# Decoder layer with routed experts: routing's normalisation written two half batches later, full-array matmuls written ahead of the values, zero rows written one transfer at a time

## The chip, the core and the metric

The kernel runs on one core of a Trainium2 chip. The metric is the device time of one execution in microseconds; the time before is the median of three runs.

## The reference

One pre-norm decoder layer on 64 sequences of 128 tokens of width 128, in float32. Two attention blocks with 16 heads of width 8 (self attention, and cross attention over a context of 77 tokens) are followed by a mixture of 8 experts, of which each token uses the best two:

```python
x = x + attn(layernorm(x))                     # 16 heads of 8
x = x + xattn(layernorm(x), ctx, mask)         # 77 keys, mask of ones
x = x + ffn(layernorm(x))

def ffn(x):                                    # E = 8, F = 512, top 2
    proj = x @ Wp.T
    gate = l2norm(proj) @ l2norm(sim).T / temperature
    top_v, top_i = top_k(gate, 2)
    comb = sum(one_hot(top_i) * softmax(top_v)[..., None], axis=-2)
    h = gelu(einsum('bsd,edf->ebsf', x, W1) + b1)
    eo = einsum('ebsf,efd->ebsd', h, W2) + b2
    return einsum('ebsd,bse->bsd', eo, comb)
```

## The kernel before

**Stages.** The 64 sequences form 16 groups of four (a sequence is called a batch in the code). First comes attention: 16 jobs of self attention and then 16 of cross attention, one job a group, 128 batches in all, in one software pipeline. Then `experts` computes the expert products for the rows of groups 0 to 10 (part 0, 51 tiles of 256 rows), and once more for groups 11 to 15 (part 1, 27 tiles). Results are gathered back and added (`gather`); the gathers of part 0 run beside the products of part 1.

**The pipeline of attention.** Step s has two halves, called half batches here. In each half `score_tiles` (S) computes two of the four head groups of batch s as scores with queries on the partitions (`ps`), and two head groups of batch s - 4 as scores with keys on the partitions (`pt`), with matmuls of 32 rows that alternate. DVE takes the row maxima `m` from `ps` (L648); they are transposed (`pm`, L659) and brought by DMA into a spare row of the queries (`qh<-md`), so that `pt` comes out shifted, and ACT takes its exponential `e` (L675). `values` (V, L690) multiplies `e` of batch s - 5 with the values, and in the other half with ones to get the sums; in every second step DVE takes the reciprocal of the sums and the product (L698, L699). `ps` and `pt` have two PSUM banks each: the next S starts when the maxima and exponentials of the last are done.

Besides S and V, each half holds some full-array matmuls, called F here: one item of the queue `todo` (taken by `next_`) and at most one of the queue `late`. `todo` holds the prologue of a job that is one to two groups ahead (normalise, transpose, query, key, value), the transposing of maxima (`turn`) and the output projection of two batches (`project`, `py`, L707). The prologue's normalise has no matmul: POOL subtracts and scales (`xn`, L170), and in self attention also takes the inverse root of the variance behind DVE's statistics (L148, L149). A group's `project` comes twice (p = 0 and 1); after p = 1 of either attention come the residual sum `xs` (L711), the statistics (L148, L149) and POOL's inverse root `rstd` (`root`, L154 to L158).

**Routing.** After p = 1 of a cross group, `route(g)` gives a function `norm` and four steps. `norm` is four DVE instructions (L170, tile `x`, buffers `x3`), called at once. The steps are queued in `late` with due times of 3, 4, 6 and 8 half batches: `trans` (transposes, an ACT copy), `project` (`pp`, squares on ACT, inverse root on POOL), `choose` (`pg`, a run of small DVE instructions for the best two), `place` (`pr`, the rows' slots). `place` fills `sending` with eight scatters, of which each half takes one: an indirect DMA of POOL that writes 128 rows into the expert rows `xr` in DRAM, written to follow the newest exponential.

When the last group of a part is placed, `table` computes from the counts which expert each tile of 256 rows belongs to and where each expert's rows end (`tail`), and then writes 256 zero rows behind the end of each of the 8 experts: a register load on SP and a DMA from `zero_s`, eight times. For part 0 this is in attention; for part 1 it is in the first expert stage, where the remaining steps of the last group are run by the function `more`, one item every second tile.

**Order.** TensorE's (PE's) instructions run in the order in which the code writes them (`manual_schedule`). The order of the others is drawn up when the program is compiled, from dependences and estimated times; the written order decides between those that are ready. In `experts` each tile's row fetch on SP is placed behind the last SP transfer of the same chain (`behind("SP")`), as are the zero writes:

```python
with behind("SP"):
    row = nc.sync.value_load(part.row[0:1, t : t + 1], ...)
i = nc.sync.dma_start(v["x"], part.x[bass.ds(row, TILE), :]...)
after(i.ins, part.scatters)
last["SP"] = i.ins
```

Rows are fetched three tiles ahead of their product.

Of the kernel before, what the change touches and what calls it, by code (L numbers as in the profile page):

```python
# [8 lines left out]
F32 = mybir.dt.float32  # L9
# [13 lines left out]
NEG = -(2.0 ** 100)  # L23
LAG = 4
TILE = 256
LATER = (3, 4, 6, 8)
SPLIT = 11


# [1 line left out]
def decoder_layer(  # L31
# [217 lines left out]
    def route(g):  # L249
# [121 lines left out]
            after(i.ins, behind)  # L371
            part.scatters.append(i.ins)

        def table():

            pn = ps_m.tile([P, E], F32, tag="mm", name="pn")
            nc.tensor.matmul(pn, ones_f, part.seen, start=True, stop=True)
            M = part.rows // TILE
            N = part.tiles
            over = hp.tile([P, E, M], F32, tag="over", name="over", bufs=1)  # L380
            need = hp.tile([P, M], F32, tag="need", name="need", bufs=1)
            nc.vector.tensor_scalar(need, tid[:, :M], float(TILE), None, ALU.mult)
            count = hp.tile([P, E], F32, tag="count", name="count", bufs=1)
            nc.vector.tensor_copy(count, pn)
            nc.vector.tensor_tensor(
                over, count.unsqueeze(2).to_broadcast([P, E, M]),
                need.unsqueeze(1).to_broadcast([P, E, M]), ALU.is_gt,
            )
            nt = hp.tile([P, E], F32, tag="nt", name="nt", bufs=1)
            nc.vector.tensor_reduce(nt, over, AX.X, ALU.add)  # L390
            acc = hp.tile([P, E, E], F32, tag="acc", name="acc", bufs=1)
            nc.vector.tensor_tensor(
                acc, low, nt.unsqueeze(1).to_broadcast([P, E, E]), ALU.mult
            )
            end = hp.tile([P, E], F32, tag="end", name="end", bufs=1)
            nc.vector.tensor_reduce(end, acc, AX.X, ALU.add)
            past = hp.tile([1, N, E], F32, tag="past", name="past", bufs=1)
            nc.vector.tensor_tensor(
                past, tid[:1, :N].unsqueeze(2).to_broadcast([1, N, E]),
                end[:1].unsqueeze(1).to_broadcast([1, N, E]), ALU.is_ge,  # L400
            )
            ex = hp.tile([1, N], F32, tag="ex", name="ex", bufs=1)
            nc.vector.tensor_reduce(ex, past, AX.X, ALU.add)
            nc.vector.tensor_tensor(
                past, past, nt[:1].unsqueeze(1).to_broadcast([1, N, E]), ALU.mult
            )
            be = hp.tile([1, N], F32, tag="be", name="be", bufs=1)
            nc.vector.tensor_reduce(be, past, AX.X, ALU.add)
            nc.vector.tensor_tensor(be, tid[:1, :N], be, ALU.subtract)
            nc.vector.tensor_scalar(be, be, float(TILE), None, ALU.mult)  # L410
            rw = hp.tile([1, N], F32, tag="rw", name="rw", bufs=1)
            nc.vector.tensor_scalar(rw, ex, float(part.step), None, ALU.mult)
            nc.vector.tensor_tensor(rw, rw, be, ALU.add)
            part.row = hp.tile([1, N], I32, tag=f"prow{part.n}", name="prow", bufs=1)
            nc.vector.tensor_copy(part.row, rw)
            nc.vector.tensor_scalar(ex, ex, float(E - 1), float(WE), ALU.min, ALU.mult)
            part.wat = hp.tile([1, N], I32, tag=f"pwat{part.n}", name="pwat", bufs=1)
            nc.vector.tensor_copy(part.wat, ex)

            nc.vector.tensor_tensor(count, count, part.base, ALU.add)  # L420
            tail = hp.tile([1, E], I32, tag=f"tail{part.n}", name="tail", bufs=1)
            nc.vector.tensor_copy(tail, count[:1])
            for e in range(E):
                with behind("SP"):
                    r = nc.sync.value_load(
                        tail[0:1, e : e + 1], min_val=e * part.step,
                        max_val=e * part.step + part.rows,
                    )
                i = nc.sync.dma_start(
                    part.x[bass.ds(r, TILE), :].rearrange("(h p) d -> p h d", p=P), zero_s  # L430
                )
                last["SP"] = i.ins
                apart(i.ins, f"x{part.n}")
                part.scatters.append(i.ins)

            K = part.last - part.first
            every = slice(part.first * GB, part.last * GB)
            less = hp.tile([P, E], F32, tag="less", name="less", bufs=1)  # L440
            nc.vector.tensor_scalar(
                less, nt, -float(TILE), float(part.step), ALU.mult, ALU.add
            )
            sf = slot_f[:, every, :].rearrange("p b k -> p (b k)")
            off = hp.tile([P, 2 * GB * SPLIT], F32, tag="off", name="off")[:, : 2 * GB * K]
            one = hp.tile([P, 2 * GB * SPLIT], F32, tag="one", name="one")[:, : 2 * GB * K]
            nc.vector.tensor_copy(off, sf)
            for e in range(1, E):
                nc.vector.tensor_scalar(
                    one, sf, float(e * part.step), less[:, e - 1 : e], ALU.is_ge, ALU.mult  # L450
                )
                nc.vector.tensor_tensor(off, off, one, ALU.subtract)
            nc.vector.tensor_copy(back[:, every, :].rearrange("p b k -> p (b k)"), off)

        return norm, [trans, project, choose, place], table if g == part.last - 1 else None

    last, newest, sending = {}, [None], []

    def behind(engine):
        return tc.issue_after(last[engine]) if engine in last else nullcontext()  # L460
# [14 lines left out]
    def attention():  # L475
        jobs = [(cross, g) for cross in (False, True) for g in range(NGRP)]
        NB = len(jobs) * GB
        with (
# [222 lines left out]
            def project(n, p):  # L701
                cross, g = jobs[n]
                v = G[n]
                wo_ = co_s if cross else wff_s
                py = ps_m.tile([P, 2, D], F32, tag="mm", name="py")
                for k in range(2):
                    nc.tensor.matmul(  # L707
                        py[:, k, :], v["aT", p][:, k, :], wo_, start=True, stop=True
                    )
                at = slice(2 * p, 2 * p + 2)  # L710
                nc.vector.tensor_tensor(xs[g][:, at, :], py, xs[g][:, at, :], ALU.add)  # L711
                if p == 1:
                    stats(g)
                    root(g)
                    v.clear()
                    if cross:
                        norm, steps, table = route(g)
                        norm()
                        late.extend((now[0] + w, f) for w, f in zip(LATER, steps))
                        if table:  # L720
                            late.append((0, table))

            loads(0)
            for f in prologue(0):
# [8 lines left out]
            for s in range(NB + LAG + 3):  # L733
                a, t, z = s, s - LAG, s - LAG - 1
                if s % GB == 2 and s // GB + 2 < len(jobs):
                    todo += prologue(s // GB + 2)
                if s == GB:
                    load_experts()
                do_a, do_t = a < NB, t in range(NB)
                for half in range(2):  # L740
                    far = (0, 1) if half == 0 else (2, 3)
                    near = (2, 3) if half == 0 else (0, 1)
                    score_tiles(a if do_a else None, far, t if do_t else None, near)
                    for x, y in zip(far, near):
                        if do_a:
                            maxima(a, x)
                        if do_t:
                            exps(t, y)
                    if z in range(NB):
                        values(z, half == 1)  # L750
                    next_()

                    now[0] += 1
                    if late and late[0][0] <= now[0]:
                        late.pop(0)[1]()
                    if sending:
                        sending.pop(0)([newest[0]])
                if len(todo) > 4:
                    next_()
                if a < NB and a % 2:  # L760
                    todo.insert(0, lambda n=a // GB, p=a % GB // 2: turn(n, p))
                if z in range(NB) and z % 2:
                    todo.insert(1, lambda n=z // GB, p=z % GB // 2: project(n, p))
# [113 lines left out]
    with tc.manual_schedule(engines={mybir.EngineType.PE}):  # L877
# [3 lines left out]
        with (  # L881
# [4 lines left out]
            def more(t):  # L886
                if rest and t % 2 == 1:
                    rest.pop(0)()
                if sending:
                    sending.pop(0)([newest[0]])  # L890

            experts(parts[0], ff, ps_h, ps_y, more)
            assert not rest and not sending
            done = [(g, b) for g in range(SPLIT) for b in range(GB)]

            def some(t):
# [68 lines left out]
```

## Time and profile before

| | |
|---|---|
| Median of 3 runs | 1540.02 us (1536.16 to 1541.31) |
| Profiled execution | 1553.91 us, of which the span is 1552.2 |
| Mean granted TensorE clock | 0.887 |
| PE busy in the span | 1301.2 us (84%) |
| DVE, ACT, POOL busy | 757.7, 530.0, 578.5 us |

By stage, from windows of the profile:

| Stage | us | PE busy | DVE busy | POOL busy | granted clock |
|---|---|---|---|---|---|
| self attention, 99 to 491 | 392 | 379.05 | 272.36 | 132.21 | 1.00 |
| cross attention, 491 to 1106 | 615 | 543.99 | 294.55 | 266.10 | 0.87 |
| experts of part 0, 1106 to 1310 | 204 | 195.72 | 81.25 | 15.71 | 0.97 |
| experts of part 1 and gathers, 1310 to 1552 | 242 | 126.72 | 77.89 | 124.62 | 0.74 |

Rows of a timeline or of the waits give the start and length in us, the engine, the line of the kernel, the operation, output and input tiles, the shapes and the number of merged instructions; in brackets stands how long the engine was idle just before and who released it. Ends of matmuls are modelled. A row of windows gives the stretch, its length, then for PE, its weight loads, DVE, ACT and POOL the busy time with the number of instructions, and at the end the granted clock, the DMA engines' busy share and GB/s.

### The profile page before, as it was taken

The page shows a single profiled execution, that of the slowest core. Times are in us where ns is not written, and L with a number is a line of the kernel's source. Part 1 is how long each engine was busy: PE and PEld are TensorE (multiplying, and loading weights), DVE is VectorE, ACT ScalarE, POOL GpSimd, SP SyncE. Part 2 cuts the span into 40 slices and gives each one's busy share as a digit, 9 for nine tenths or more (in the row PEclk, how much of TensorE's full clock was granted, in tenths as well). Part 3 has the DMA queues.
Part 4 walks back from the last instruction along what each step waited for, and adds up shares of the span by engine and source line. Part 5 has one row for each costly group of instructions (what it writes and reads, how often), then busy time and mean ns, then how long its engine had stood idle before and what let it go on. Part 6 is the DMA issues. An engine that isn't in the chain of part 4 may idle for free.

```text
span 1552.2 us, 47623 instructions
## 1 busy us (share of the span) xinstructions
PE 1301.2 (84%) x20147; PEld 1032.1 (66%) x20147; DVE 757.7 (49%) x2094; ACT 530.0 (34%) x1167; POOL 578.5 (37%) x928
## 2 busy tenths in 40 slices
PE   1889999999999999999999998988679999555940
PEld 1667777777777666666666666666579999444840
DVE  2347767767765454444444445444343333333422
ACT  1134444444444333333333333323334444111410
POOL 5404243342523244444444443334410001666136
PEclk9589999999999899898989898878789999687975
DMA  7542212122221111111111112101132222333212
GB/s 196 132 91 52 53 40 60 40 53 50 43 53 40 34 45 47 48 47 46 47 44 49 42 47 69 39 16 36 41 94 75 69 75 73 89 90 93 83 51 71
DMA packets 120213, 95.58 MB, mean 62 GB/s; under 512 B 22584, under 2 KB 102592, under 8 KB 120000
## 3 DMA queue, kind: packets, MB, share of 16 engines
q1 hardware_dynamic: 97328, 58.73, 15.5%
q0 software_dynamic: 8192, 16.79, 3.8%
q10 hardware_dynamic: 14480, 17.02, 3.6%
q8 instruction: 158, 2.59, 0.7%
q14 instruction: 55, 0.45, 0.1%
HBM read 49.60 MB, written 42.89 MB: 60 GB/s over the span
## 4 chain that ended last, share of the span: by engine, by line
PE 68%; POOL 11%; issue 7%; DVE 6%; DMA 4%; another core or an unknown queue 2%; SPq 1%; POOLq 0%; ACT 0%; DVEq 0%
PE po L690 14%; PE ps L629 13%; PE py L824 7%; PE ph L806 7%; PE pt L629 4%; PE pt L638 4%; PE py L707 3%; PE ps L638 3%; POOL rstd L154 3%; POOL xn L170 3%; POOL r L858 2%; PE pq L567 2%; PE pv L593 2%; PE pk L579 2%
## 5 line engine op out<-in xcount | busy, mean ns | idle before, releaser
L675 ACT ACTIVATE e<-pt 128x512 f32<-128x512 f32 (+1 forms) x512 | 279.2, 592 | 382.1 <-PE pt L638 236.3
L629 PE MATMUL ps<-kh,qh 31*128 31x128 f32 (+1 forms) x4096 | 346.1, 299 | 64.2 <-DVE m L648 51.3
L648 DVE TENSOR_REDUCE m<-ps 128x4 f32<-128x512 f32 (+1 forms) x512 | 275.8, 578 | 252.8 <-PE ps L638 125.6
L629 PEld LDWEIGHTS ps<-kh,qh 31*128 31x128 f32 x4096 | 294.2, 202 | 136.1 <-DVE m L648 82.2
L629 PE MATMUL pt<-qh,kh 32*128 32x128 f32 (+1 forms) x4096 | 334.5, 293 | 7.0 <-DMA qh<-md 5.2
L629 PEld LDWEIGHTS pt<-qh,kh 32*128 32x128 f32 (+1 forms) x4096 | 268.5, 173 | 11.3 <-issue 10.1
L858 POOL DMA_INDIRECT r<-yr,back x128 | 124.6, 974 | 257.0 <-DMA xr<-xr 150.7
L365 POOL DMA_INDIRECT xr<-x,slot x128 | 129.0, 1008 | 236.0 <-ACT e L675 148.9
L813 ACT ACTIVATE hT<-ph,wr 128x256 f32<-128x256 f32 x312 | 128.9, 471 | 248.0 <-issue 227.2
L806 PE MATMUL ph<-xT,wr 128*128 128x256 f32 x624 | 162.2, 407 | 27.8 <-DVE xT L798 11.6
L824 PE MATMUL py<-wr,hT 128*128 128x128 f32 x1248 | 164.2, 283 | 24.7 <-issue 24.4
L824 PEld LDWEIGHTS py<-wr,hT 128*128 128x128 f32 x1248 | 160.7, 200 | 33.7 <-issue 29.0
L690 PE MATMUL po<-e,ones_w 128*32 128x128 f32 (+1 forms) x4096 | 155.5, 292 | 2.6 <-issue 1.8
L806 PEld LDWEIGHTS ph<-xT,wr 128*128 128x128 f32 x624 | 121.1, 204 | 46.7 <-DVE xT L798 12.8
L690 PE MATMUL po<-e,vm 128*32 128x128 f32 (+1 forms) x4096 | 141.9, 278 | 1.3 <-issue 1.1
L690 PEld LDWEIGHTS po<-e,ones_w 128*32 128x32 f32 (+1 forms) x4096 | 113.9, 116 | 39.9 <-issue 31.3
L698 DVE RECIPROCAL aT<-po 128x256 f32<-128x256 f32 x64 | 112.5, 1757 | 41.1 <-PE po L690 40.2
L690 PEld LDWEIGHTS po<-e,vm 128*32 128x32 f32 (+1 forms) x4096 | 105.4, 110 | 31.2 <-issue 24.0
L170 POOL TENSOR_SCALAR xn<-xs,stat,rstd 128x128 f32<-128x128 f32 x128 | 103.6, 818 | 56.3 <-PE tp L184 54.4
L830 DVE TENSOR_TENSOR yr<-py,wr 128x256 f32<-128x256 f32 x78 | 33.0, 424 | 179.4 <-PE py L824 140.0
L163 POOL TENSOR_SCALAR var<-stat 128x4 f32<-128x4 f32 x48 | 11.3, 235 | 259.2 <-DVE stat L149 257.3
L638 PE MATMUL pt<-ident_b,bias 128*77 128x512 bf16 x256 | 100.3, 408 | 0.0
(163 smaller groups left out, 1383.5 us busy)
## 6 DMA issues: line engine op xcount, KB each, us to landing
xr<-xr SPq DMA_DIRECT2D x78, 128.0 KB
yr<-yr SPq DMA_DIRECT2D x78, 128.0 KB
d<-qT ACTq DMA_DIRECT2D x32, 256.0 KB
qh<-d SPq DMA_DIRECT2D x128, 64.0 KB
xs<-in_x_dram SPq DMA_DIRECT2D x16, 256.0 KB
d<-kT ACTq DMA_DIRECT2D x16, 256.0 KB
kh<-d SPq DMA_DIRECT2D x64, 64.0 KB
we_s<-in_w_dram SPq DMA_DIRECT2D x16, 256.0 KB
```

The costliest lines, as they stand in the source:

```text
L170: (engine or nc.gpsimd).tensor_scalar(xn[:, b, :], xs[g][:, b, :], stat[:, i, 0:1], rstd[:, i : i + 1], ALU.subtract, ALU.mult,)
L365: i = nc.gpsimd.indirect_dma_start(out=part.x, out_offset=bass.IndirectOffsetOnAxis(ap=slot[:, g * GB + b, k : k + 1], axis=0), in_=v["xn" ...
L629: nc.tensor.matmul(pt[:, r, :], v[still][rows, r, b, :], v[moving][rows, r, b, :], start="bias" not in v or r == 0, stop="bias" not in v,)
L638: nc.tensor.matmul(pt, left, right.unsqueeze(1).to_broadcast([P, HG, K]), start=False, stop=True,)
L648: nc.vector.tensor_reduce(v["m", b // 2][:, c, :, b % 2], v.pop(("ps", b, c)), AX.X, ALU.max, negate=True,)
L675: i = nc.scalar.activation(e[:K], pt[:K], AF.Exp)
L690: nc.tensor.matmul(po[32 * c : 32 * c + 32, :], w[:, 32 * j : 32 * j + 32], v["e", b, c][:K, j, :], start=(j == 0), stop=(j == HG - 1),)
L698: nc.vector.reciprocal(r, v["o"][:, 1])
L806: nc.tensor.matmul(ph[:, c % 2, :], v["w"][:, c * P : (c + 1) * P], v["xT"], start=True, stop=True,)
L813: i = nc.scalar.activation(v["h"][:, n, :], ph[:, n % 2, :], AF.Gelu, bias=v["w"][:, WF + n : WF + n + 1],)
L824: nc.tensor.matmul(py[:, h, :], v["h"][:, c, h * P : (h + 1) * P], v["w"][:, F + c * D : F + (c + 1) * D], start=(c == 0), stop=(c == NFC ...
L858: inst = nc.gpsimd.indirect_dma_start(out=r, out_offset=None, in_=part.y, in_offset=bass.IndirectOffsetOnAxis(ap=back[:, i, k : k + 1], ax ...
```

## The change

Three edits. First, `norm` is no longer called at once after `project`, but becomes the first of five entries in `late`, with a due time of 2 half batches; since the queue is looked at right after the count goes up, it is written one half after the projection, behind that half's scores and `next_`. Second, in each half `values` moves behind `next_` and the item of `late`: S V F becomes S F V. Third, `table` becomes a function of its own outside `route`, and its eight zero writes go into a new queue `clearing`, of which each half (and in `more` each tile) takes one. The computations of `table` are the same; its text is only moved.

```diff
-LATER = (3, 4, 6, 8)
+LATER = (2, 3, 4, 6, 8)
...
+        return [norm, trans, project, choose, place]
+
+    def table(part):
...
-            for e in range(E):
-                with behind("SP"):
-                    r = nc.sync.value_load(
-                        tail[0:1, e : e + 1], min_val=e * part.step,
-                        max_val=e * part.step + part.rows,
-                    )
-                i = nc.sync.dma_start(
-                    part.x[bass.ds(r, TILE), :].rearrange("(h p) d -> p h d", p=P), zero_s
-                )
-                last["SP"] = i.ins
-                apart(i.ins, f"x{part.n}")
-                part.scatters.append(i.ins)
+        def tail_zeros(e):
+            with behind("SP"):
+                r = nc.sync.value_load(
+                    tail[0:1, e : e + 1], min_val=e * part.step,
+                    max_val=e * part.step + part.rows,
+                )
+            i = nc.sync.dma_start(
+                part.x[bass.ds(r, TILE), :].rearrange("(h p) d -> p h d", p=P), zero_s
+            )
+            last["SP"] = i.ins
+            apart(i.ins, f"x{part.n}")
+            part.scatters.append(i.ins)
+
+        clearing.extend(lambda e=e: tail_zeros(e) for e in range(E))
...
-        return norm, [trans, project, choose, place], table if g == part.last - 1 else None
-
-    last, newest, sending = {}, [None], []
+    last, newest, sending, clearing = {}, [None], [], []
...
                     if cross:
-                        norm, steps, table = route(g)
-                        norm()
-                        late.extend((now[0] + w, f) for w, f in zip(LATER, steps))
-                        if table:
-                            late.append((0, table))
+                        late.extend((now[0] + w, f) for w, f in zip(LATER, route(g)))
+                        if g == parts[g >= SPLIT].last - 1:
+                            late.append((0, lambda: table(parts[g >= SPLIT])))
...
-                    if z in range(NB):
-                        values(z, half == 1)
                     next_()
 
                     now[0] += 1
                     if late and late[0][0] <= now[0]:
                         late.pop(0)[1]()
+                    if z in range(NB):
+                        values(z, half == 1)
                     if sending:
                         sending.pop(0)([newest[0]])
+                    if clearing:
+                        clearing.pop(0)()
...
                 if sending:
                     sending.pop(0)([newest[0]])
+                if clearing:
+                    clearing.pop(0)()
```

## The prediction

> **What bounds it now.** I read the waits first, then the timelines of DVE and PE around one of them, then windows of the granted clock, then SP. The waits of the whole span name one chain:
>
> ```profile
> DVE x L170 <- POOL rstd L158: 48.2, 16, 8.7
> PE ps L629 <- DVE m L648: 51.3, 30, 6.1
> ```
>
> Routing's normalisation x waits 16 times, once a cross group, for POOL's inverse root; PE's scores wait for the maxima m. DVE, then PE, in group 5 show that it is one chain:
>
> ```profile
> 707.43 0.42 DVE L711 TENSOR_TENSOR xs<-py,xs 128x256 f32<-128x256 f32 x1 [2.45 <-PE py L707]
> ...
> 711.21 1.12 DVE L170 TENSOR_SCALAR x<-xs,stat,rstd 128x128 f32<-128x128 f32 x4 [2.61 <-POOL rstd L158]
> 712.24 0.86 DVE L648 TENSOR_REDUCE m<-ps 128x4 f32<-128x308 f32 x2
> ```
> ```profile
> 709.75 0.28 PE L659 MATMUL pm<-ident,m 128*32 128x128 f32 x1
> 712.77 0.34 PE L629 MATMUL ps<-kh,qh 31*128 31x77 f32 x1 [2.74 <-DVE m L648]
> ```
>
> DVE is in order: m stands behind x, and PE idles 2.74 us. The windows (PE busy second, granted clock third from the end) show the larger price:
>
> ```profile
> 712.00:713.00 1.00, 0.23 (x4) 0.23 (x4) 1.00 (x4) 0.00 (x0) 0.80 (x1) 0.98 0.00 0
> 713.00:714.00 1.00, 1.00 (x20) 0.96 (x21) 0.10 (x1) 0.00 (x0) 0.00 (x0) 0.50 0.26 82
> ...
> 723.00:724.00 1.00, 1.00 (x12) 0.41 (x11) 0.51 (x2) 0.29 (x1) 0.00 (x0) 0.90 0.00 0
> ```
>
> From 712.98 to 723.2 PE runs at half clock. Every cross group repeats this: groups 1 to 10 have periods of 38.0 to 40.2 us (mean 39.2), a gap of 2.74 (group 1: 3.03), then 6.8 or 10.2 us at half clock. The longer phase makes the period 1.75 us longer for 3.4 us more of half clock, so the loss is 0.51 of it: 4.3 us on average. The clock changes only on a grid of 3.41 us. Which idle time trips it:
>
> ```profile
> 552.50:555.90 3.40, 2.08 (x38) 1.24 (x37) 0.87 (x5) 1.34 (x3) 1.99 (x6) 1.00 0.26 63
> 555.90:559.30 3.40, 1.68 (x34) 1.49 (x35) 1.93 (x6) 0.00 (x0) 1.20 (x2) 1.00 0.10 29
> 559.40:562.80 3.40, 3.40 (x38) 2.24 (x37) 1.15 (x3) 1.19 (x2) 0.96 (x1) 0.50 0.02 6
> ```
>
> 1.32 us idle in one grid window kept the clock, 1.72 in the next lost it; a gap of 1.69 at 1403.4, all in one window, kept it. So some 1.7 us, half a window, decides.
>
> The Trainium skill (TensorE: Matmul & The Clock Gate, Part 1) has the free-running window of about 3.4 us, but asks for a whole idle window or a gap over some 3 us. By that 2.74 us would cost no clock and the cross part below would be 13 x 1.5 = 20 us instead of 73; the trace, with a drop after every 2.74, decides against it.
>
> The second wait lies in the first expert stage:
>
> ```profile
> 1133.25 8.83 SPq L429 DMA_DIRECT2D xr<-zero  x8
> 1142.91 0.40 SPq L780 DMA_DIRECT2D xr<-xr  x1
> ```
> ```profile
> 1145.24 0.66 PE L796 MATMUL tp<-ident,xr 128*128 128x128 f32 x2 [7.95 <-DMA xr<-xr]
> ```
>
> Eight zero writes go ahead of a row fetch on SP, and PE waits 7.95 us.
>
> **Does x move?** PE follows the written order; the other engines' order is drawn up at compile time by readiness. The self stage proves it:
>
> ```profile
> 266.52 0.27 DVE L148 BATCH_NORM_STATS2 st<-xs 128x6 f32<-128x128 f32 x1
> 266.70 0.30 DVE L149 BATCH_NORM_AGGREGATE stat<-st 128x2 f32<-128x6 f32 x2
> 266.92 1.25 DVE L648 TENSOR_REDUCE m<-ps 128x4 f32<-128x512 f32 x2
> ```
>
> Of the eight statistics of a period, four belong to a prologue written after these maxima and the next ones, and still run ahead of both. x needs only xs, its statistics and rstd, nothing from the halves that it is moved past. So I expect x to stay ahead of m: the new due time does nothing by itself. No instruction is added or removed anywhere.
>
> **Part 1: full-array work F ahead of the values V.** Cross halves go from S V F to S F V. Between py (the p = 1 projection) and the second score block after it stands one V more (1.01 us), so POOL gets that lead. Counted from the end of py's own score block (704.57): now py at 1.0, xs at 2.86, x at 6.64, the blocked scores at 8.2, PE ready for them at 5.46. After: py at 0, xs at 0.8 (py to xs takes 0.75 without scatters, group 0), statistics end 1.2 later, POOL's second scatter ends at 2.0 to 2.2, the root takes 2.5: x at 4.8, scores 1.56 later at 6.4; PE is ready at 4.9 to 5.46. Gap 0.9 to 1.5; I take 1.2, under 1.7: the clock stays. xs now starts 1.1 us late, just behind a scatter of 0.96; were that repeated, the gap would be 2.74 again (upper bound). The lower bound is 0.
> Groups 1 to 10: (2.74 - 1.2) + 4.3 = 5.8 each, 58. Group 0 (gap 2.28, 10.2 us at half clock): 6. Group 12: 7. Groups 11 (6.06, with the table's own DVE work ahead of m) and 13 (3.85) stay above 1.7: 1 each. Sum **-73**.
>
> In the self stage the same order costs. There F waits for POOL:
>
> ```profile
> 274.54 0.33 PE L184 MATMUL tp<-ident,xn 128*128 128x128 f32 x1 [0.45 <-POOL xn L170]
> ```
>
> Now V fills most of that wait; afterwards V comes behind it. xs must still wait for the 1.29 us of maxima, so its chain (xs, statistics, two roots, four xn of 0.79: 9.67 us) starts only 0.34 earlier against 1.01 for F: +0.67 a group. The reciprocal and product behind V (1.76 + 0.42) now begin with the next S and hold its maxima until 3.6 us after its start, where PE wants the bank at 3.2: +0.4. Cross scores are longer (1.86 against 1.10) and cover this. 13 groups with such a chain: 13 x 1.07 = **+14** (bounds 0 and 25). DVE and ACT get F's results a V earlier; ACT's copies follow the exponentials in both orders: nothing.
>
> **Part 2: zero rows singly.** SP's fetches and zero writes are chained in written order, so a fetch now passes seven of the eight writes (1.1 us each); beside a tile of 3.73 us, one write, one fetch (0.40) and one store (0.41) fit. The 7.95 goes, with 2.2 lost at half clock until 1149.6: **-10**. What is late next is the tail table on DVE (1132.47), with the fetch at about 1134.3, three tiles ahead as always. In attention (946.12 to 954.7) they block only qh<-md, whose scores come two batches later: nothing.
>
> Sum: -73 + 14 - 10 = **-69**. The profiled execution took 1553.91 (span 1552.2): 1485. The median of the runs is 1540.02, 0.991 of it: **1472**. Own range of this case 1457 to 1492.
>
> **Rivals.**
> *x does move behind m* (the due time works): the gaps of 1.2 vanish too, 13 x 1.2 = 16 more: 1456. For it: a lower rank in ties. Against: the statistics above. 0.12.
> *The gap stays over half a window*: xs is held by the scatter as today. Then +14 - 10: 1544, or a little below if some groups escape. For it: xs starts 0.68 us behind that scatter's end in group after group. Against: py would be done before the scatter begins. 0.16.
> *The self stage loses its clock*: its four transposes stretch over 2.3 us, 1.6 of it idle. If transposing counted as idle, 2.3 passes 1.7 in about 0.7 of the phases: 13 x 0.7 x 4.3 = 39: 1511. For it: nothing in these rows tells transposes from idle time. Against: today's 1.26 us of the same keeps 1.00. 0.12.
> The Trainium skill (same page, Part 4) says that transposes do not count as PE-busy in the same way: this rival is that rule, and no row here decides it.
> *The clock trips lower, near 1.2 us* (slower): then the cross gap still trips it (only 13 x 1.5 = 20 gained), and the self wait of 1.6 newly does (39 lost): -20 + 14 + 39 - 10 = +23, 1563. Against: the kept windows of 1.32 and 1.69. It decides as soon as 1.2 to 1.6 idle is enough. 0.08.
>
> **How the numbers follow.** My case has 0.52. The range 1450 to 1538 takes in the third rival and the edge of the second, and leaves out the slow rival, most of the second and a little below: about 0.2. A measurement of this kernel tells 0.3% (4.6 us) from nothing. Faster: 0.52 + 0.12 + 0.12 + 0.04 = 0.80; same 0.06 and slower 0.06 from the second rival, with 0.08 from the last: 0.14.
>
> **What would show it.** Right: x still between stat and m on DVE with its POOL wait; PE's gap 0.9 to 1.5 and clock 1.00 in cross groups, periods near 33; self periods 25.2 to 25.6 against 24.5 with a longer xn wait; zero writes and fetches alternating after 1060, no gap of 8. Wrong: half clock still in each cross group, or any in the self stage; or x behind m.

## The result and the profile after

The changed kernel takes 1452.91 us (median of 4 runs, 1451.14 to 1455.83) against 1540.66 for the kernel before beside it (4 runs, 1536.16 to 1543.02): a ratio of 0.9436, 95% interval 0.9409 to 0.9462. The forecast was 1472, range 1450 to 1538. The profiled execution took 1452.79 us (span 1451.1), almost its median; that of before, 1553.91 us, lay 13 us above its own, so the two traces differ by 101 us where the medians differ by 88.

The wait at the head of the prediction, in the changed kernel's chain of waits (total, times, longest):

```profile
DVE x L170 <- POOL rstd L158: 41.2, 13, 5.9
```

It is still there, a little shorter. What follows from it is smaller, as DVE's and then PE's timeline in group 5 shows:

```profile
679.64 0.42 DVE L713 TENSOR_TENSOR xs<-py,xs 128x256 f32<-128x256 f32 x1
...
683.74 1.11 DVE L170 TENSOR_SCALAR x<-xs,stat,rstd 128x128 f32<-128x128 f32 x4 [2.93 <-POOL rstd L158]
684.76 0.86 DVE L650 TENSOR_REDUCE m<-ps 128x4 f32<-128x308 f32 x2
```
```profile
685.29 0.33 PE L631 MATMUL ps<-kh,qh 31*128 31x77 f32 x1 [1.39 <-DVE x L170]
```

x stands where it stood, ahead of m, and still waits for POOL. But PE's gap is 1.39 where it was 2.74: PE has one V more to do in the meantime. Counted from the end of py's own score block (679.00), x starts at 4.74 us and the blocked scores at 6.29, and PE is ready for them at 4.90. Groups 0 to 10 have gaps of 1.29 to 1.42 (mean 1.37); a period is 32.14 us against 39.22 (means from group 2 to group 10).

The clock is not quite kept. In windows on its grid of 3.41 us (granted clock third from the end), group 5 and then group 7:

```profile
683.86:687.28 3.42, 2.03 (x40) 1.67 (x37) 1.98 (x7) 0.00 (x1) 1.11 (x1) 1.00 0.09 29
687.28:690.69 3.41, 3.41 (x22) 2.88 (x24) 1.53 (x6) 1.44 (x3) 0.96 (x1) 0.50 0.10 24
...
748.70:752.12 3.42, 2.13 (x38) 1.75 (x37) 1.98 (x7) 0.13 (x1) 1.11 (x1) 1.00 0.13 36
752.12:755.53 3.41, 3.41 (x77) 3.02 (x75) 2.10 (x7) 1.53 (x3) 0.96 (x1) 1.00 0.24 66
```

1.39 us idle in one window cost the next window half its clock; 1.29 cost nothing. Of groups 0 to 10, five lose a window; one is the kept 1.29, and in the other five the grid cuts the gap, with at most 1.09 us in one window. A fall lasts one window, where it was two or three before.

The self stage pays for the order, and keeps its clock, 1.00 from 100 to 500 us. Six of its periods before and after as windows, then PE's timeline after:

```profile
204.23:351.23 147.00, 140.45 (x3232) 108.90 (x3236) 104.76 (x229) 69.34 (x132) 51.26 (x102) 1.00 0.21 49
205.51:356.81 151.30, 144.98 (x3236) 110.85 (x3232) 104.87 (x229) 67.43 (x132) 51.20 (x102) 1.00 0.21 47
```
```profile
276.72 0.33 PE L184 MATMUL tp<-ident,xn 128*128 128x128 f32 x1 [0.45 <-POOL xn L170]
277.50 0.33 PE L184 MATMUL tp<-ident,xn 128*128 128x128 f32 x1 [0.44 <-POOL xn L170]
```

The transposes now wait twice for POOL where they waited once, and a period is 25.22 us (sums xs at 281.16 and 306.38) against 24.50. But PE is not idle for longer: 1.05 us a period against 1.09, because the scores' wait for the maxima m, 0.5 us once a period before, is gone. PE's busy time grew, from 23.41 to 24.16 us a period, with the same matmuls at the same clock. From start to start, the block of four transposes, of which the last three now wait for their xn one by one, takes 2.24 us where it took 1.26; pm takes 0.6 less, without the wait for m behind it, and the eight score blocks together 0.4 more.

On SP, in the first expert stage, zero writes and fetches take turns, and the 7.95 us is gone:

```profile
1053.02 0.39 SPq L782 DMA_DIRECT2D xr<-xr  x1
1054.19 0.38 SPq L431 DMA_DIRECT2D xr<-zero  x1
...
1056.05 0.39 SPq L782 DMA_DIRECT2D xr<-xr  x1
```

### The profile page after: what moved, and what is told of

Its sections match the earlier page's. It is cut to its first block, busy times and chain, and to the rows that moved or that the text cites. A ratio compares the mean times of both kernels' runs of the same rounds, so it can differ in the third digit from the quotient of the medians.

```text
span 1451.1 us, 47629 instructions
## 1 busy us (share of the span) xinstructions
PE 1238.6 (85%) x20147; PEld 1008.3 (69%) x20147; DVE 758.4 (52%) x2094; ACT 516.6 (36%) x1167; POOL 578.7 (40%) x928
## 4 chain that ended last, share of the span: by engine, by line
PE 64%; POOL 12%; issue 9%; DVE 7%; DMA 4%; another core or an unknown queue 2%; ACT 1%; POOLq 0%; SPq 0%; ACTq 0%; DVEq 0%
PE po L692 13%; PE ps L631 12%; PE py L826 9%; PE ph L808 8%; PE pt L631 4%; PE pt L640 3%; POOL xn L170 3%; PE ps L640 3%; POOL rstd L154 3%; PE pq L569 2%; POOL r L860 2%; DVE m L650 2%; PE pk L581 2%; PE py L709 2%
## 5 line engine op out<-in xcount | busy, mean ns | idle before, releaser
L631 PE MATMUL ps<-kh,qh 31*128 31x128 f32 (+1 forms) x4096 | 335.3, 289 | 33.7 <-DVE x L170 10.9
L631 PEld LDWEIGHTS ps<-kh,qh 31*128 31x128 f32 x4096 | 282.1, 192 | 100.3 <-DVE m L650 31.1
L631 PE MATMUL pt<-qh,kh 32*128 32x128 f32 (+1 forms) x4096 | 323.2, 283 | 4.3 <-DMA qh<-md 4.1
L631 PEld LDWEIGHTS pt<-qh,kh 32*128 32x128 f32 (+1 forms) x4096 | 256.8, 166 | 6.0 <-issue 5.3
L692 PE MATMUL po<-e,ones_w 128*32 128x128 f32 (+1 forms) x4096 | 139.5, 277 | 0.0
L692 PEld LDWEIGHTS po<-e,ones_w 128*32 128x32 f32 (+1 forms) x4096 | 104.8, 110 | 35.9 <-issue 26.7
L640 PE MATMUL pt<-ident_b,bias 128*77 128x512 bf16 x256 | 95.7, 391 | 0.0
```

The source lines that it names most:

```text
L631: nc.tensor.matmul(pt[:, r, :], v[still][rows, r, b, :], v[moving][rows, r, b, :], start="bias" not in v or r == 0, stop="bias" not in v,)
L640: nc.tensor.matmul(pt, left, right.unsqueeze(1).to_broadcast([P, HG, K]), start=False, stop=True,)
L692: nc.tensor.matmul(po[32 * c : 32 * c + 32, :], w[:, 32 * j : 32 * j + 32], v["e", b, c][:K, j, :], start=(j == 0), stop=(j == HG - 1),)
```

## Experiments

Theory: readiness keeps x ahead of m, so the due time does nothing; the order S F V gives POOL a V of cover and so shrinks the gap and what the clock loses; the zero writes are worth 10 us by themselves. The rivals are in the expectations. "us" below is the ratio times 1540.7; each kernel was timed beside the kernel before. The last column is the difference of two ratios that each have an interval, and is certain to 5 to 8 us only: the -7 of self_svf and the -5 of root_less are not told from nothing by their times, and what is said of them rests on their traces.

| Kernel | ratio (95%) | us against before | against the changed kernel |
|---|---|---|---|
| norm_late | 0.9988 (0.9964 to 1.0013) | -2 | |
| values_last | 0.9516 (0.9494 to 0.9539) | -75 | +12 |
| zeros_single | 0.9937 (0.9916 to 0.9958) | -10 | |
| x_behind | 0.9256 (0.9229 to 0.9284) | -115 | -28 |
| x_behind_svf | 0.9473 (0.9431 to 0.9515) | -81 | |
| self_svf | 0.9389 (0.9349 to 0.9429) | -94 | -7 |
| both | 0.9190 (0.9146 to 0.9234) | -125 | -38 |
| root_less | 0.9401 (0.9361 to 0.9441) | -92 | -5 |
| root_more1 | 0.9488 (0.9457 to 0.9519) | -79 | +8 |
| root_more4 | 0.9628 (0.9602 to 0.9653) | -57 | +30 |
| root_short_svf | 0.9657 (0.9613 to 0.9702) | -53 | |

**norm_late: the due time alone**

```diff
-LATER = (3, 4, 6, 8)
+LATER = (2, 3, 4, 6, 8)
...
-                        norm, *steps = route(g)
-                        norm()
-                        late.extend((now[0] + w, f) for w, f in zip(LATER, steps))
+                        late.extend((now[0] + w, f) for w, f in zip(LATER, route(g)))
```

> Of the three edits only the first: routing's normalisation is due two half batches later; values ahead of the full-array matmuls and all zero writes at once, as in the kernel before. Theory (the other engines' order is drawn up by readiness, so a later due time changes nothing where x is ready): on VectorE x stays between the statistics and the maxima m in all cross groups but the one with the table, the gaps of 2.74 us and the half clock after them stay, and the time is 1535 to 1541 us (at most a few us gained in the one group with the table, whose gap was 6.06). Rival (the due time is what frees the maxima): gaps under 1.5, full clock in the cross part, 1450 to 1470 us.

0.9988, no difference that the interval can tell. DVE, then PE, in one group:

```profile
743.84 1.11 DVE L170 TENSOR_SCALAR x<-xs,stat,rstd 128x128 f32<-128x128 f32 x4 [2.62 <-POOL rstd L158]
744.87 0.86 DVE L651 TENSOR_REDUCE m<-ps 128x4 f32<-128x308 f32 x2
```
```profile
745.39 0.49 PE L632 MATMUL ps<-kh,qh 31*128 31x77 f32 x1 [2.74 <-DVE m L651]
```

Order, wait and gap are those of before, though x is written one half batch later (that is where the due time of two puts it). The rival falls. Only the group with the table changes: x stands behind the maxima there (x from 944.49, m at 943.17 and 943.95), and its gap is 3.42 here, 6.06 before, 4.47 in values_last and 1.67 with both edits.

**values_last: the order S F V alone**

```diff
-                    if z in range(NB):
-                        values(z, half == 1)
                     next_()
                     now[0] += 1
                     if late and late[0][0] <= now[0]:
                         late.pop(0)[1]()
+                    if z in range(NB):
+                        values(z, half == 1)
```

> Only the second edit: full-array matmuls ahead of the values; the normalisation is emitted where it was before and all zero writes at once. Theory (the order S F V alone gives GpSimd one more V of cover): the cross gaps shrink to 1.3 to 1.5 us as in the changed kernel, the self period is 25.2 against 24.5, the gap of 7.95 in the first expert stage stays, and the time is some 10 to 15 us above the changed kernel: 1461 to 1470 us. Rival (the due time and the order are needed together): gaps over 2 us and half clock after each, 1530 us or more.

0.9516, 1466 us; the gaps read 1.27 to 1.41 in ordinary groups, and the wait for the fetch is 7.90. The order makes nearly the whole gain.

**zeros_single: the zero writes alone**

```diff
-            for e in range(E):
-                tail_zeros(e)
+            clearing.extend(lambda e=e: tail_zeros(e) for e in range(E))
```

> Only the third edit: zero rows written one transfer at a time. Theory: the gap of 7.95 us at the start of the first expert stage and about 2 us of half clock after it go, nothing else moves: 1540 - 10 = 1530 us. Rival (the tail table on VectorE, or the fetch three tiles ahead, ends the wait anyway): a wait of 5 us or more remains in the same place and the time is within 4 us of 1540.

0.9937, 1531 us; the trace has no wait of 2 us or more for the fetch there. The three edits by themselves are worth -2, -75 and -10, together -86 before rounding; the change has -87. They add up.

**x_behind: what is left of the gap**

```diff
         def norm():
-            v["xn"] = normalised(g, "x3", 3, nc.vector)
+            with tc.issue_after(newest_m[0]):
+                v["xn"] = normalised(g, "x3", 3, nc.vector)
...
-                nc.vector.tensor_reduce(
+                i = nc.vector.tensor_reduce(
...
+                newest_m[0] = i.ins
```

> The changed kernel, with routing's four x instructions on VectorE forced behind the newest maxima m that are already written (between m and m in place of ahead of both). Theory (x's wait for GpSimd, with m queued behind it, is all of the gap that is left): the 13 gaps of about 1.37 us go (18 us), and the windows of half clock behind seven of them (about 1.7 us each, 12 us): 1453 - 30 = 1423 us, clock 1.00 throughout the cross part. Rival (the wait moves to the transposes tp that read x, or to the next maxima behind x): a gap of 1 us or more appears behind the next scores or ahead of tp in each group, and the time stays within 8 us of 1453.

0.9256: 28 us less than the change. DVE now does what the due time was not able to bring about:

```profile
731.07 0.86 DVE L652 TENSOR_REDUCE m<-ps 128x4 f32<-128x308 f32 x2 [1.57 <-PE ps L642]
732.46 1.12 DVE L170 TENSOR_SCALAR x<-xs,stat,rstd 128x128 f32<-128x128 f32 x4 [0.52 <-DMA xr<-x,slot]
734.40 0.86 DVE L652 TENSOR_REDUCE m<-ps 128x4 f32<-128x308 f32 x2 [0.82 <-PE ps L642]
```

x runs between two pairs of maxima, and no gap of 0.5 us is left in groups 0 to 10. x itself still waits there, 0.5 to 0.6 us where it waited 2.6 to 2.9 in the changed kernel, in most groups for POOL's rstd, but no maxima stand behind the wait that PE needs next. So the wait of x, with m behind it, is all of the gap, and the rival falls. From 855 to 862 (the table's DVE work ahead of m, a gap of 1.69) and from 940 to 958 (a gap of 1.15 ahead of py) the clock is still half.

**x_behind_svf: the same in the old order**

The kernel before with the edits of norm_late and of x_behind.

> The kernel before in its order S V F and with all zero writes at once, the normalisation due two half batches later, and its four x instructions on VectorE forced behind the newest maxima m. Theory (the whole cross gain is the end of VectorE's wait ahead of m, and the order S F V adds nothing but a little): no gap and clock 1.00 in the cross groups, period about 31 to 32 us, the self part as before the change (24.5 a period): 1540 - 28 (gaps) - 58 (clock) = 1454, some 10 us less if the transition from S to F saves nothing. Second theory (in S F V each cross half is 0.2 us shorter per transition, some 1.5 us a group): then the cross period here is 32.2 against 30.8 with S F V, and the time about 1445 to 1460. Rival (in S V F the wait moves on to the next maxima, since x is ready a V later): a gap of 1 us or more in each group and 1480 us or more.

0.9473, 1459 us. No gap and a full clock here too, but a group takes 32.22 us, in x_behind 29.99. Windows over eight groups of x_behind and of x_behind_svf:

```profile
594.03:833.96 239.93, 239.31 (x4762) 192.39 (x4756) 151.77 (x521) 100.17 (x249) 152.18 (x249) 1.00 0.23 61
```
```profile
589.75:847.53 257.78, 252.43 (x4756) 188.22 (x4758) 148.96 (x520) 104.36 (x248) 150.51 (x249) 1.00 0.22 57
```

So S F V is worth 2.23 us a group without any wait of x: 0.6 of idle time ((257.78 - 252.43) - (239.93 - 239.31), by 8) and 1.6 in which PE is busy for less time with the same instructions. From start to start, S F takes less than S V: score blocks ahead of py, pv or pq 1.76 to 1.77 where they took 1.86 ahead of V (ahead of pm, pk and tp it is 1.89 to 1.94), the py behind them 0.53 for 0.64. Summed over a group, score blocks save 0.8 us, F 0.55 and the V's 0.9, of which 0.8 lies in one place: in the old order the V ahead of pq takes 1.83 us on average where the others take 1.01, and the idle time in and behind it is put down to "issue", that is, to nothing that the profile shows. The second theory was right in kind and too small (it had 30.8). Why PE takes less time in this order was not tried; in the self stage the same order makes it busy for longer.

**self_svf and both: the self stage as before**

```diff
+                    if z in range(NB // 2):
+                        values(z, half == 1)
                     next_()
...
-                    if z in range(NB):
+                    if z in range(NB // 2, NB):
                         values(z, half == 1)
```

> The changed kernel with the values ahead of the full-array matmuls again in the self stage alone. Theory (what the order costs in the self stage is 0.715 us a period, 13 periods): self period 24.5 again, cross part unchanged, 1453 - 9 = 1444 us. Rival (the loss of 7 us up to the cross part lies in the start-up or in the hand-over from self to cross): self period 24.5 but under 3 us gained, 1450 us or more.

0.9389, 1447 us; the period is 24.50 again, with PE busy for 23.41 us of it as before. The time alone does not tell the theory's 9 us from the rival's under 3. In the trace the xs of cross group 0 comes at 507.93 us where it came at 519.15 in the changed kernel, so the theory is right on the self stage; but the span is only 6 us shorter, and the cross part and the experts thus gave some 5 back. `both` has this and the forced x:

> The changed kernel with x forced behind the newest maxima m, and values ahead of the full-array matmuls in the self stage. Theory (the two gains lie in different stages and add up): 28 us from the first (x_behind measured 0.9256 against 0.9436) and 9 from the second: 1416 us, ratio 0.919 to the kernel before. Rival (the half-clock windows fall anew on another phase of their 3.41 us grid and take the second gain back): 1425 us or more.

0.9190, 1416 us (median 1420.51 beside 1545.76): the fastest of all, and the two gains add up.

**root_less, root_more1, root_more4: the length of the gap, in the order S F V**

The first leaves out the addition of the small constant to the variance in cross groups, the others add instructions that add zero:

```diff
-            v = work.tile([P, GB], F32, tag="var", name="var")
-            nc.gpsimd.tensor_scalar(v, stat[:, at, 1], EPS, None, ALU.add)
+            v = stat[:, at, 1]                        # root_less, cross only
...
+            for _ in range(k if cross else 0):        # root_more: k = 1 or 4
+                nc.gpsimd.tensor_scalar(v, v, 0.0, None, ALU.add)
```

> The changed kernel with one GpSimd instruction less (0.3 us) ahead of the inverse root in cross groups: the addition of the small constant to the variance is left out there. It shortens POOL's part of x's wait and nothing else. Theory (in the cross part the clock is lost where 1.29 to 1.34 us of idle time or more lies in one window of 3.41 us): gaps of 1.07 us, no window of half clock in groups 0 to 10; 13 x 0.3 = 4 us of gap and about 7 x 1.7 = 12 us of clock gained: 1437 us. Rival (the clock has no such edge, and falls with a chance that grows with the gap): still four or more windows at half clock, and 1445 us or more.

0.9401, 5 us less instead of 16: gaps of 1.00 on average, and three of groups 0 to 10 still lose a window. So the theory's edge of 1.29 to 1.34 is wrong, and the rival's numbers are nearer (five windows with groups 11 and 12, and 1448 us). But it does not look like chance. Two windows of this kernel and what follows each:

```profile
584.84:588.26 3.42, 2.41 (x65) 1.97 (x59) 1.89 (x6) 0.71 (x3) 1.33 (x3) 1.00 0.18 43
588.26:591.67 3.41, 3.41 (x16) 2.82 (x15) 1.14 (x3) 1.19 (x2) 0.96 (x1) 0.50 0.01 5
745.27:748.68 3.41, 2.44 (x39) 2.06 (x40) 1.97 (x7) 0.46 (x1) 0.95 (x1) 1.00 0.10 32
748.68:752.10 3.42, 3.42 (x77) 2.94 (x76) 2.08 (x6) 1.21 (x3) 0.96 (x1) 1.00 0.26 70
```

Busy for 2.41 and 2.44 us, and one falls and the other doesn't. What PE did in them besides the 32 row-tiled scores, first in the one that falls (groups by line):

```profile
L694 PE MATMUL po<-e,vm 77*32 77x128 f32 x32 | 1.1, 276 | 0.0
```
```profile
L642 PE MATMUL pt<-ident_b,bias 128*77 128x512 bf16 x2 | 0.7, 379 | 0.0
...
L597 PE MATMUL pv<-cv_s,ctx 128*77 128x128 f32 x3 | 0.5, 272 | 0.0
```

The first holds values, in tiles of 32 columns, and almost no full-array work; the second holds the bias matmuls and part of pv. This sorts all nine windows of the cross groups of this kernel with 0.97 to 1.05 us idle: the four that fall (the last in group 12) hold 28 to 32 values and at most two bias matmuls, the five that don't hold 0 to 20 values and four bias matmuls.

> The changed kernel with one GpSimd instruction of some 0.28 us more ahead of the inverse root in cross groups, so that the gap is about 1.65 us. Theory (the edge of the clock lies at 1.0 to 1.35 us of idle time in one window, lower where the window holds only row-tiled scores and values): most groups fall to half clock for one window, about 10 instead of 6 of groups 0 to 10: 13 x 0.28 + 4 x 1.7 = 10 us more, 1463 us. Rival (1.7 us decides, as forecast from the kernel before): no more windows than now, 3.6 us more, 1457 us.

0.9488, 8 us more, nearer to the theory's 10 than to the rival's 3.6: gaps of 1.65, seven of groups 0 to 10 lose a window where five did (expected were ten; in the others the grid cuts the gap). The windows speak against the rival more surely than the time does.

> The changed kernel with four GpSimd instructions of some 0.28 us more ahead of the inverse root in cross groups (they add zero), so that x is ready 1.1 us later and the gap is about 2.5 us again, in the order F ahead of V. Theory (the length of the gap alone sets what the clock costs, as before the change: two or three windows of 3.41 us, 4.3 us a group): a period of 30.0 + 2.5 + 4.3 = 36.8 us against 32.1, 1453 + 13 x 4.6 = 1513 us. Rival (with F ahead of V the half clock lasts one window whatever the gap): a period of 30.0 + 2.5 + 1.7 = 34.2, 1453 + 13 x 2.1 = 1480 us.

0.9628, 30 us more: the rival. Gaps of 2.55, each group from 0 to 10 falls, mostly for one window and at times two, at a period of 34.76. With nearly the gap of before (2.74), before's 39.22 does not come back. One window fell where nothing was changed: in the self stage, which is that of the changed kernel, the clock is 0.51 from 226.88 to 230.29, behind a window with 0.99 us idle that held all four transposes, 32 scores and ten values. The self stage thus stands at the edge too: in the six traces of this order, 44 of its windows have 0.95 to 1.05 us idle, and this one alone fell.

**root_short_svf: the shorter gap in the old order**

```diff
+        if cross:
+            nc.gpsimd.tensor_tensor(rstd[:, at], stat[:, at, 1], half_s, ALU.pow)
+            return
```

> The kernel before in every respect, its order S V F too, but in cross groups GpSimd's inverse root is the power alone: the addition of the small constant and the Newton step (five instructions, some 1.4 to 1.5 us) are left out, so that x is ready that much earlier and the gap of 2.74 us becomes about 1.3 us, the gap that the changed kernel has with S F V. Theory (the order sets how long the half clock lasts: with values right behind the scores it stays down for two or three windows once it falls): period 32.2 + 1.3 + 2 to 4 = 35.5 to 37.5 us against 39.2, 1540 - 13 x 2.7 = 1505 us, at least 1490. Rival (the length of the gap sets it: one window, in about half of the groups): period 32.2 + 1.3 + 0.8 = 34.3, 1540 - 13 x 4.9 = 1476 us.

0.9657, 1488 us, between the two and nearer to the rival's 1476 and its period (34.35 for 34.3). But it gets there in another way: only three of groups 0 to 10 fall at all, and those falls last two or three windows, as the theory said. One of them:

```profile
754.91:758.33 3.42, 3.42 (x37) 2.31 (x35) 0.81 (x2) 0.59 (x1) 0.00 (x0) 0.50 0.05 13
758.33:761.74 3.41, 3.41 (x40) 2.93 (x40) 1.26 (x2) 0.60 (x2) 0.96 (x1) 0.50 0.06 19
761.74:765.15 3.41, 3.41 (x41) 2.86 (x40) 1.70 (x6) 0.59 (x1) 0.00 (x0) 0.50 0.19 46
765.15:768.57 3.42, 3.42 (x56) 2.66 (x58) 0.86 (x2) 1.77 (x4) 1.59 (x2) 1.00 0.07 22
```

PE is busy for every bit of the first two windows, and the clock does not come back. The largest group rows of the second, and of the one window at half clock at 687.28 in the changed kernel, which was enough:

```profile
L693 PE MATMUL po<-e,ones_w 77*32 77x128 f32 x32 | 1.9, 421 | 0.0
L596 PE MATMUL pv<-cv_s,ctx 128*77 128x128 f32 x7 | 1.8, 432 | 0.0
```
```profile
L595 PE MATMUL pv<-cv_s,ctx 128*77 128x128 f32 x8 | 1.9, 421 | 0.0
L184 PE MATMUL tp<-ident,x 128*128 128x128 f32 x4 | 1.1, 421 | 0.0
L692 PE MATMUL po<-e,ones_w 77*32 77x128 f32 x8 | 0.6, 398 | 0.0
```

In the order S V F the values come between the scores and pv; in S F V, pv and tp follow the scores at once and fill the window.

**The six cross periods side by side** (means over eight ordinary groups; "without" is the period without gap and loss, from x_behind_svf and x_behind; "clock" is the period less the gap and less "without"):

| Order | kernel | gap | period | without | clock |
|---|---|---|---|---|---|
| S V F | before | 2.74 | 39.22 | 32.22 | 4.26 |
| S V F | root_short_svf | 1.29 | 34.35 | 32.22 | 0.84 |
| S F V | root_more4 | 2.55 | 34.76 | 29.99 | 2.22 |
| S F V | root_more1 | 1.65 | 32.86 | 29.99 | 1.22 |
| S F V | changed | 1.37 | 32.14 | 29.99 | 0.78 |
| S F V | root_less | 1.00 | 31.85 | 29.99 | 0.86 |

"clock" is a remainder: in periods in which no window falls it still is some 0.2 us. And it is an average over groups that fall and groups that don't: of the eight, one falls in root_short_svf, three in the changed kernel and in root_less, five in root_more1, all in root_more4 and before.

The change's 7.08 us a group is 2.23 (the order itself) + 1.37 (gap) + 3.48 (clock).

## Why the prediction was right, point by point

- *x stays ahead of m, and the due time does nothing by itself.* Right, and norm_late shows it. The exception was not foreseen: in the group with the table x did move, and its gap fell from 6.06 to 3.42 by the due time alone. With both edits the gap is 1.67, so 4.4 us went there where the sum had 1.
- *Part 1, the gap.* Forecast 0.9 to 1.5, taken 1.2; measured 1.37. Right, and by the path that was forecast: x at 4.74 (forecast 4.8), the scores at 6.29 (6.4), PE ready at 4.90 (4.9 to 5.46). The order alone brings it (values_last), and the gap follows the length of POOL's work: 1.00, 1.37, 1.65 and 2.55 with one instruction less, none, one and four more.
- *Part 1, "under 1.7: the clock stays".* Wrong. That edge was read from three windows of before, whose content was not looked at; the kept 1.69 stood between full-array matmuls of the experts. Five of groups 0 to 10 fall at 1.34 to 1.42, and in root_less at 1.0. This costs some 0.8 us a group where nothing was charged. The slow rival had the lower edge nearly right, but not what hung on it: a fall lasts one window in the new order, and the self stage does not fall in the changed kernel.
- *Part 1, the sum for groups 1 to 10: 5.8 each.* The period fell by 7.08. The term that was missing is the 2.23 that S F V saves without any wait; the clock's 3.48 is less than the 4.3 in the sum, and the gap's 1.37 less than 1.54. These misses are of opposite sign, and the first is larger: the sum is 13 us short here ((7.08 - 5.8) x 10). The part that was forecast, gap and clock, gave 4.85 of the 5.8; that the total lies above it and not below is not the prediction's merit.
- *The self stage, 13 x 1.07 = 14.* Right in sign and place, too large: 13 x 0.72 = 9.3 by the periods (7 by self_svf, which is not clear of noise). The two terms were not what it is made of. The block that waits for xn grew by 0.98, not 0.67. The other, maxima held by the reciprocal so that PE waits 0.4 longer for them, has the wrong sign: PE's wait for m, 0.5 before, is gone. The rest, 0.4 in the score blocks, was not foreseen, and no run shows what causes it.
- *Part 2, -10.* Right: -10 alone (zeros_single), and from the first product of part 0 to the first of part 1 it is 193.8 us in the trace of after, 203.8 in that of before.
- *Profile to median.* By the traces the change saves 101 us where the sum had 69. Of the 32 that it is short, 11 lie in groups 0 to 10, 10 in groups 11 to 13 (of which two were given 1 us each), 8 ahead of the xs of cross group 0, which is the self stage above all, and the rest behind. The step to the median, which took 13 us off 1485, made 19 of it: the trace of before lay 13 us above its median, and that of after does not. Without this step the forecast would have been 32 us too high: that it came within 19 is partly luck.
- *Rivals.* x does not move behind m; made to, it gives 28 us, not the 16 forecast for it, because the half-clock windows go with the gaps. The gap does not stay over half a window: xs is not held by the scatter. The self stage of the changed kernel keeps 1.00 throughout, so its transposes did not cost it its clock; the one window that fell in root_more4 shows that it was near. The Trainium skill (TensorE: Matmul & The Clock Gate, Part 4) does not count transposes in transpose mode as PE-busy in the same way. The self stage does not bear that out: with its transposes (1.0 to 1.3 us) counted as idle, the 44 windows with 0.95 to 1.05 us idle would have 1.9 us or more, and 43 of them kept the clock, where the changed kernel's cross windows fell from 1.34 on; but no run took the transposes out.

## What to carry to other kernels

An in-order engine that waits for a slow producer ahead of work that another engine needs can be relieved in two ways: give the producer more time, or put the wait behind that work. The later due time did neither, as the order was drawn up by readiness; naming the instruction to follow did it and was worth 28 us more. And a gap on TensorE is priced by what stands around it: 2.74 us cost 4.3 us of clock with the values behind the scores, and 2.55 cost 2.2 with full-array matmuls behind them. A change of order is to be measured in each stage by itself: this one saved 2.23 us a group in the cross part and cost 0.72 a period in the self stage, both mostly in PE's busy time and not in its waits.

## What the runs showed of the hardware that was not expected

- Idle time alone does not decide the clock. In root_less, windows with 0.99 to 1.02 us idle fell where the rest was row-tiled scores and values, and windows with 0.97 to 1.05 did not where they held all four bias matmuls; in the changed kernel 1.29 was kept and 1.34 lost. It looks as if matmuls on a part of the array count for less. This sorts the windows, but no run changed only the kind of the matmuls, and in the self stage one window fell with 0.99 us idle where others of nearly the same content did not.
- A PE that is busy for a whole window need not get its clock back: 3.42 and 3.41 us busy in two windows running, at 0.50 after both. The Trainium skill (TensorE: Matmul & The Clock Gate, Part 1) has the full clock after one busy window of about 3.4 us; the rows of root_short_svf go against that for windows with many row-tiled matmuls.
- The order of the same matmuls on PE changes how long they take: 2.23 us in 32.22 less in the cross groups and 0.72 in 24.50 more in the self stage, with a full clock in all four.
